# Rotary sine product in one VectorE instruction, and decay factors completed on ScalarE

## The chip, the cores and the metric

The kernel runs on one core of a Trainium2 chip. The time is device microseconds of one execution, the median over repeated runs. The engines are TensorE (PE, with its weight loads PEld), VectorE (DVE), ScalarE (ACT), GpSimd (POOL) and the queue engine SyncE (SP). Each takes its instructions in order, and they wait for each other through semaphores.

## What is computed

The input `x` has 32 sequences of 256 tokens with 256 features, all in float32. A state-space block, conditioned by a vector per sequence, comes first, then two layers of windowed attention with a gated feed-forward, and the input is added to the end. Cut to what the change touches:

```python
# state-space block: one decay factor per state (16) and token
dt = jnp.tanh(dt @ W_dt.T + b_dt) * 0.01
A = -jnp.tanh(A_log)
Ad = 1.0 + dt * A
def step(h, inputs):
    ad, bd, xt, ct = inputs
    h = jnp.clip(h * ad[:, :, None] + bd[:, :, None] * xt[:, None, :], -10.0, 10.0)
    return h, jnp.einsum('bd,bdh->bh', ct, h)
...
# attention: rotary embedding of q and k, heads of 64
def rotate_half(x):
    x1, x2 = jnp.split(x, 2, axis=-1)
    return jnp.concatenate([-x2, x1], axis=-1)
q = q * cos * scale + rotate_half(q) * sin * scale
k = k * cos / scale + rotate_half(k) * sin / scale
```

## The kernel before, in words

The 32 sequences are worked on in 4 groups of 8. The scan of a group takes 256 steps, one per token, in 8 chunks of 32. A step holds the states of 8 sequences x 16 states on 128 partitions and 512 features, and is one VectorE instruction (`step`, L722), which reads the former state and the token's row `xrep`, already spread by a DMA and scaled on ScalarE (`scale_row`, L712); TensorE reads four states out at a time (L734). For each chunk a preparation runs ahead of the steps: convolution (L474 to L514), layer norm and projections, and then the factors of the chunk.

These factors are where the first edit lies. `figures_in` (L636 to L644) makes the inputs `bcd` on VectorE, `decay_th` (L649) takes the tanh of 128x32 values on ScalarE, and `decays` multiplies it by a value per partition and adds 1 on VectorE (L654). A scan instruction (L656) makes the running product `pd`, and L659 to L663 its reciprocal `pi`, the scaled `beta` and `ct`. Each row of the chunk is scaled by `beta` on ScalarE before its step. `decay_th` stands in slot -6 before its chunk and `decays` in slot -5, where a slot is one step of the scan.

The second edit lies in the attention, which works on one sequence after another, for 2 layers. TensorE projects one window of 128 tokens to q or k in a PSUM bank (L996, 128x512: 8 heads of 64). `rotated` squares it on ScalarE (L1009), multiplies it by the cosine table on VectorE (L1012, into `rot`), and then by the sine table with the halves of each head exchanged, in two VectorE instructions of 128x256 (L1017, into `swp`). GpSimd adds the two (L1020). VectorE sums the squares (L1022), GpSimd raises the sums to -1/2 (L1026), and VectorE scales `rot` with that (L1032). That is done 4 x 8 x 2 x 2 x 2 = 256 times. The sign of the rotation is in the sine table. `swp` and the squares share three buffers with the end result `fo`, and a PSUM bank comes free when its last reader, L1017, has ended.

The program text says which slot of the scan and which stage of the attention work stands in: the scan of group 0 runs alone, then the attention of one group runs beside the scan of the next, and the attention of the last group runs alone. But the text is not the order of the queues. A planner takes the instructions at build time and writes each engine's order from its own costs, taking at each point the first in program order that it holds to be ready. `keep_in_program_order` pins some instructions behind their predecessors (L712 in the later groups, L1032). An instruction that is added, dropped or has another cost can so change the order on every engine. Other lines named further on: L588/L589 and L764 are GpSimd products and sums of 128x512, L1423 and L1443 finish the feed-forward on VectorE, L1060 adds the attention's output.

## Time and profile before

| | |
|---|---|
| median of 3 runs | 3534.1 us (3530.1 to 3535.7) |
| the profiled execution | 3535.6 us, span of its instructions 3533.5 us |
| granted TensorE clock | 0.99 of full speed |
| L654, factor on VectorE | 32 x 570 ns |
| L649, tanh on ScalarE | 32 x 318 ns |
| L1012, cosine product, 128x512 | 256 x 684 ns |
| L1017, sine product, 128x256 | 512 x 416 ns |
| L1020, addition on GpSimd, 128x512 | 256 x 1348 ns |
| L722, scan step | 1024 x 896 ns |

A row of the profile names the line, engine, operation, output and inputs, the shapes and the count; behind the bar come the busy time in us, the mean ns of one instruction, then the idle time of its engine just before such instructions and what ended it. The chain of waits goes back from the last instruction, at each step to what released it or to the instruction before it on its engine; "issue" in it is time in which the profile shows nothing that the engine waited for. TensorE's busy time is modelled and covers short gaps.

### The profile page before, as it was taken

The numbers are of one execution on the slowest core, as the hardware profiler recorded it, in microseconds if no ns is written. First come the engines' busy times: TensorE is split into PE (matmuls) and PEld (weight loads), VectorE is DVE, ScalarE is ACT, GpSimd is POOL, SyncE is SP. The second block draws the span as 40 slices with busy tenths as digits, with TensorE's granted clock in tenths as the row PEclk, the third lists the DMA queues.
The fourth block names the chain that finished last, engine by engine and source line by source line (L and its number), as shares of the span: only waits on it lengthen the run. The fifth ranks groups of instructions, "written<-read, shape, count | busy, mean of one in ns | idle before, by whom it ended". The sixth has DMA issues, their size and how long they took to land.

```text
span 3533.5 us, 56484 instructions
## 1 busy us (share of the span) xinstructions
PE 3418.2 (97%) x19580; PEld 2257.4 (64%) x19580; DVE 2683.2 (76%) x5177; ACT 2035.4 (58%) x3663; POOL 1625.6 (46%) x1587
## 2 busy tenths in 40 slices
PE   7999989999999999999999999999999999999999
PEld 4545335666666666666666666666666777777777
DVE  5888898878788788888888888888787655555563
ACT  4666656656666665666666656666566444444442
POOL 4433456544455555544455555544444434333441
PEclk9999999999999999999999999999999999999999
DMA  7787655545454555444454555544444212011111
GB/s 208 215 217 218 198 169 153 136 113 142 129 143 130 150 147 151 136 114 134 117 142 128 148 148 147 137 120 130 118 142 118 61 37 62 13 31 36 37 28 38
DMA packets 487195, 436.65 MB, mean 124 GB/s; under 512 B 247155, under 2 KB 326516, under 8 KB 486772
## 3 DMA queue, kind: packets, MB, share of 16 engines
q1 hardware_dynamic: 401426, 420.41, 42.2%
q10 hardware_dynamic: 85474, 12.53, 2.1%
q8 instruction: 157, 2.57, 0.3%
q14 instruction: 138, 1.13, 0.1%
HBM read 384.06 MB, written 47.19 MB: 122 GB/s over the span
## 4 chain that ended last, share of the span: by engine, by line
PE 63%; DVE 17%; DMA 7%; POOL 5%; ACT 4%; issue 3%; SPq 1%; ACTq 0%; DVEq 0%; POOLq 0%
PE ps_qkv L996 13%; PE pa L1405 13%; DVE h L722 7%; PE po_f L1432 6%; PE y L734 5%; PE ps_wo L1052 4%; PE ov L1289 3%; DMA xrep<-xnd 3%; PE ps_out L814 3%; PE ps_in L401 3%; PE sc L1232 3%; PE tr_qk L1041 2%; PE rs L1269 2%; PE ps_raw L520 2%; DVE acc L491 1%
## 5 line engine op out<-in xcount | busy, mean ns | idle before, releaser
L722 DVE CUSTOM_DVE_ANT_0 h<-h,xrep,lim 128x512 f32<-128x512 f32 x1024 | 917.2, 896 | 137.3 <-ACT xrep L712 93.4
L712 ACT ACTIVATE xrep<-xrep,beta 128x512 f32<-128x512 f32 x960 | 671.6, 719 | 265.5 <-DMA xrep<-xnd 178.2
L996 PE MATMUL ps_qkv<-qkv,res 128*128 128x512 f32 x1536 | 716.0, 601 | 26.6 <-DVE ag L1423 12.5
L1405 PE MATMUL pa<-hT,w 128*128 128x256 f32 (+1 forms) x2816 | 674.7, 382 | 5.1 <-DVE zT L805 5.1
L1405 PEld LDWEIGHTS pa<-hT,w 128*128 128x128 f32 (+1 forms) x2816 | 517.4, 188 | 145.4 <-issue 41.8
L1020 POOL TENSOR_TENSOR rot<-rot,swp 128x512 f32<-128x512 f32 x256 | 345.1, 1348 | 496.7 <-DVE swp L1017 465.9
L996 PEld LDWEIGHTS ps_qkv<-qkv,res 128*128 128x128 f32 x1536 | 282.0, 191 | 311.5 <-issue 247.0
L1026 POOL TENSOR_TENSOR rn<-ss,neg_half 128x8 f32<-128x8 f32 x256 | 457.6, 1788 | 0.0
L734 PE MATMUL y<-h,ly 128*32 128x512 f32 x2048 | 341.1, 606 | 15.7 <-DVE h L722 13.6
L1432 PE MATMUL po_f<-ag,w 128*128 128x256 f32 x1280 | 306.7, 387 | 3.8 <-DVE fo L1443 3.1
L1423 DVE SCALAR_TENSOR_TENSOR ag<-pa,b_sb,ag 128x256 f32<-128x256 f32 x320 | 151.5, 474 | 208.7 <-ACT ag L1416 208.7
L1009 ACT ACTIVATE sq<-ps_qkv,tiny 128x512 f32<-128x512 f32 x256 | 173.3, 685 | 186.3 <-PE ps_qkv L996 129.3
L1432 PEld LDWEIGHTS po_f<-ag,w 128*128 128x128 f32 x1280 | 235.3, 190 | 68.3 <-DVE pT L1260 12.9
L1416 ACT ACTIVATE ag<-pa,b_sb 128x256 f32<-128x256 f32 x320 | 150.0, 469 | 209.7 <-PE pa L1405 206.8
L1357 POOL TENSOR_TENSOR rstd<-ve,neg_half 128x2 f32<-128x2 f32 x64 | 46.5, 726 | 484.9 <-DVE ve L1355 484.8
L1052 PE MATMUL ps_wo<-oT,wo 128*128 128x256 f32 x1024 | 231.6, 379 | 0.0
L1012 DVE TENSOR_TENSOR rot<-ps_qkv,rc_sb 128x512 f32<-128x512 f32 x256 | 175.1, 684 | 71.8 <-ACT sq L1009 70.1
L491 DVE SCALAR_TENSOR_TENSOR acc<-xr,wc_sb,acc 128x256 f32<-128x256 f32 x384 | 183.1, 499 | 50.8 <-POOL acc L480 50.0
L1017 DVE TENSOR_TENSOR swp<-ps_qkv,rs_sb 128x256 f32<-128x256 f32 x512 | 191.8, 416 | 27.6 <-POOL rot L1020 27.5
L1052 PEld LDWEIGHTS ps_wo<-oT,wo 128*128 128x128 f32 x1024 | 194.5, 190 | 27.2 <-ACT th_g L774 0.8
L1032 DVE SCALAR_TENSOR_TENSOR rot<-rn,rot 128x512 f32<-128x512 f32 x256 | 205.7, 841 | 7.5 <-POOL rn L1026 7.5
L1244 ACT ACTIVATE pT<-sc 128x512 f32<-128x512 f32 x384 | 201.6, 601 | 8.2 <-PE sc L1232 6.1
(161 smaller groups left out, 5375.6 us busy)
## 6 DMA issues: line engine op xcount, KB each, us to landing
xrep<-xnd SPq DMA_DIRECT2D x960, 256.0 KB
rb<-inv SPq DMA_DIRECT2D x128, 256.0 KB
xnd<-xn SPq DMA_DIRECT2D x64, 256.0 KB
qkv<-in_wqkv_dram SPq DMA_DIRECT2D x24, 512.0 KB
ahead<-xs_a SPq DMA_DIRECT2D x48, 256.0 KB
xp<-ahead SPq DMA_DIRECT2D x48, 256.0 KB
xd<-xnd SPq DMA_DIRECT2D x192, 64.0 KB
w<-in_w_dram SPq DMA_DIRECT2D x80, 128.0 KB
```

The source lines that it names most:

```text
L491: nc.vector.scalar_tensor_tensor(acc, xr[:, :, k : k + CH], wc_sb[:, ch, k : k + 1], acc, ALU.mult, ALU.add,)
L712: scaled = nc.scalar.activation(bx, ck[c].pop(("bx", t), bx), AF.Copy, scale=ck[c]["beta"][:, t : t + 1])
L722: nc.vector._custom_dve(TENSOR_ADD_SAT, out=h_new, in0=state["h"], in1=bx, s0=ck[c]["lim"][:, 0, t : t + 1], s1=ck[c]["lim"][:, 1, t : t + 1],
L734: nc.tensor.matmul(ck[c]["y", hb][32 * q : 32 * q + 32, :], ly[hb % 2][:, 32 * t : 32 * t + 32], ck[c].pop(("h", hb * TB + t)), start=(i = ...
L996: nc.tensor.matmul(ps, res[b][:, k, t0 : t0 + W], wt["qkv", a][:, k], start=(k == 0), stop=(k == KM - 1),)
L1020: nc.gpsimd.tensor_add(rot, rot, swp)
L1026: nc.gpsimd.tensor_tensor(rn, ss, neg_half, ALU.pow)
L1032: nc.vector.scalar_tensor_tensor(rot, bc(rn, 2, DH), 1e12, rot, ALU.min, ALU.mult)
L1052: nc.tensor.matmul(po[:, d], wt["wo", 0][:, c, d * P : (d + 1) * P], oT[:, c, :], start=(c == 0), stop=(c == NC_ - 1),)
L1244: nc.scalar.activation(p, banks[r], AF.Exp)
L1405: nc.tensor.matmul(dst[x], wt["w1", m][:, k, x], self.h[:, k], start=(k == 0), stop=(k == KM - 1),)
L1432: nc.tensor.matmul(self.po[:, d], wt["w2", 0][:, m, d * P : (d + 1) * P], self.ag[m], start=(m == 0), stop=(m == len(MCH) - 1),)
```

## The change

The two sine products become one of 128x512. It reads the PSUM bank as (head, half, 32) with the halves backwards, and the table and the output in their plain order. And ScalarE computes `1 + a * tanh` itself, in place, in an activation (Identity, with a scale and a bias per partition) directly behind the tanh; VectorE's instruction for it is gone.

```diff
             def decay_th(c):
                 ad = sm.tile([P, CH], FP, tag="ad", name="ad")
                 nc.scalar.activation(ad, ck[c]["bcd"][:, 2], AF.Tanh, bias=wbias[:, 2:3])
+                nc.scalar.activation(ad, ad, AF.Identity, bias=one, scale=a_sb)
                 ck[c]["ad"] = ad
 
             def decays(c):
                 ad, bcd, beta = ck[c].pop("ad"), ck[c].pop("bcd"), ck[c]["beta"]
-                nc.vector.tensor_scalar(ad, ad, a_sb, 1.0, ALU.mult, ALU.add)
...
             hd = DH // 2
-            for i in range(2):
-                o, s = slice(i * hd, (i + 1) * hd), slice((1 - i) * hd, (2 - i) * hd)
-                nc.vector.tensor_mul(
-                    swp[:, :, o], ph[:, :, s], bc(rs_sb[:, l, w, a, o], 1, HEADS)
-                )
+
+            nc.vector.tensor_mul(
+                swp.rearrange("p h (i d) -> p h i d", i=2),
+                ps.rearrange("p (h i d) -> p h i d", h=HEADS, i=2)[:, :, ::-1, :],
+                bc(rs_sb[:, l, w, a].rearrange("p (i d) -> p i d", i=2), 1, HEADS),
+            )
```

## The prediction

> **What bounds the kernel now.** I read the page's busy shares first, then the busy time by stage, then the chain of waits through one period of the middle stage, and last the timeline of VectorE (DVE) around the lines that change.

> ```profile
> PE 3418.2 (97%) x19580; PEld 2257.4 (64%) x19580; DVE 2683.2 (76%) x5177; ACT 2035.4 (58%) x3663; POOL 1625.6 (46%) x1587
> ```

> The second view is the busy time of each engine in three stretches (PE, PEld, DVE, ACT, POOL in that order, then the granted clock, the DMA share and GB/s).

> ```profile
> 100.00:400.00 300.00, 283.86 (x1244) 149.95 (x1242) 261.19 (x455) 195.77 (x360) 115.61 (x156) 0.95 0.79 217
> 1700.00:2600.00 900.00, 879.26 (x5165) 593.63 (x5162) 748.16 (x1474) 558.67 (x1020) 453.55 (x423) 1.00 0.48 134
> 2700.00:3500.00 800.00, 799.97 (x4711) 581.60 (x4704) 448.59 (x861) 356.73 (x606) 297.20 (x234) 1.00 0.16 42
> ```

> There are three stages. Behind 2700 us TensorE (PE) has no gap at all, so nothing that VectorE saves there counts. In the middle PE idles 20.7 of 900 us (2.3%), and from 100 to 400 us 16.1 of 300. Over the whole span it idles 3533.5 - 3418.2 = 115 us, and that is the most that a faster VectorE could ever return. The middle repeats itself every 100 us, once per chunk of the scan. Its chain of waits (start, length, what) has these pieces:

> ```profile
> 1744.76 0.72 DVE h L722
> 1745.48 0.09 DVE ad L654
> 1745.57 1.00 issue
> 1746.57 0.80 DVE h L722
> 1747.37 0.20 DVE pd L656
> ...
> 1765.10 0.60 DVE rot L1012
> 1765.70 0.67 DVE swp L1017 x2
> 1766.38 0.03 issue
> 1766.40 0.02 POOLq L1020
> 1766.42 0.09 issue
> 1766.51 1.28 POOL rot L1020
> 1767.79 0.02 issue
> 1767.81 0.07 DVE swp L1017
> ```

> Both edited lines are on the chain: the decay's L654, and the sine products L1017 with the GpSimd addition L1020 that waits for them. Summing the chain's pieces by line over the whole span gives 39.2 us for L1017 (120 pieces) and 3.6 us for L654 (19 pieces). So the change touches the path that sets the end, but little of it.

> **Part 1, the sine product.** The duration of a row is not its price, because one VectorE instruction starts before the one in front has ended. The timeline (start, length) shows it:

> ```profile
> 1765.03 0.68 DVE L1012 TENSOR_TENSOR rot<-ps_qkv,rc_sb 128x512 f32<-128x512 f32 x1
> 1765.63 0.73 DVE L1017 TENSOR_TENSOR swp<-ps_qkv,rs_sb 128x256 f32<-128x256 f32 x2
> 1766.29 0.67 DVE L1022 TENSOR_REDUCE ss<-sq 128x8 f32<-128x512 f32 x1
> ```

> The two halves hold the engine from 1765.63 to 1766.29, 0.66 us. The cosine product L1012 has the same sources (PSUM and a broadcast table in SBUF) and 512 elements, and holds it from 1765.03 to 1765.63, 0.60 us. The new instruction is a product of that size, so one pair saves 0.06 to 0.07 us; over all rows the mean start-to-start time is 333 ns for a half, and 600 to 609 ns for a whole L1012. I take 0.066 us, or 17 us of VectorE in 256 pairs. On the chain it is 39.2 / 0.333 = 118 halves, 59 pairs, **3.9 us**. No row reads with a negative step. The halves read runs of 32 at a stride now, in 333 ns, like the unbroken 256-element sum L474 (334 to 336 ns), and L805 writes a strided output in 0.60 us, so I give the pattern nothing. By the bare durations, 2 x 416 - 684 = 148 ns a pair, the same 59 pairs would give 8.7 us; that end I keep for the range. What waits behind the pair (L1020's addition, the PSUM bank that the scores' matmuls take) gets its data 0.07 us sooner, inside the same sum. The second product of a window waits for L1020 of the first (0.26 us in the same view) and will still do so.

> [...]

> **Part 2, the decay factor on VectorE.** Its group row and that of the tanh in front of it:

> ```profile
> L654 DVE TENSOR_SCALAR ad<-ad,a_sb 128x32 f32<-128x32 f32 x32 | 18.2, 570 | 8.6 <-ACT ad L649 8.6
> ```

> 570 ns is a mean of two things. 20 of the 32 take 223 to 242 ns, and 10 take 1245 to 1261 ns; in all ten GpSimd had begun L764 (a product of two SBUF tensors) 0.2 to 0.4 us before, and the 1.00 us of "issue" in the chain is this hold. Start to start an undisturbed one costs 0.15 to 0.25 us. On the chain: **3.6 us** over 19 pieces, without the holds. Are the holds gained as well, 10 x 1.0 us? The next instruction on VectorE is the scan step L722, which reads two SBUF tensors and is itself seen between 715 and 1896 ns (median 807). So it can be held too, and would then stand in the same place until L764 ends. I count none of the 10 us and keep them as the far end.

> [...]

> From 100 to 450 us the tanh comes late: L654 waited 0.3 to 2.0 us for it at five chunks and 0.5 at a sixth, together 6.9 us, with step L722, whose input may be ready, standing behind it. Now only the scan L656 waits, and L722 lies between. Bounds: 0 (the step is not ready, its rows still on the DMA queue) and 6.9; neither row is nearer, so I take half, **3.5 us**.

> **Part 3, the factor on ScalarE.** 32 new activations of 128x32. The tanh of the same shape takes 318 ns (L649) and reads the same kind of operands, so +0.32 us each, 10 us of ScalarE in all. A ScalarE instruction directly behind the one that feeds it exists (L574, then L581): its wait for L574 sums to 0.4 us in 64, so none is added. Identity is used by L581 and L1383 already with no table load of its own, so no load either. Queued behind it on ScalarE is the row scaling L712, for which the scan step waits. What covers it: ScalarE waits 3.4 us for L638 in front of the tanh and 3.5 us for L660 a few instructions later, once per chunk, and the tanh is on the chain in only 4 pieces. Cost: 4 x 0.32 = **1.3 us**; if that cover is gone, 32 x 0.32 = 10 us.

> No DMA is issued, removed or moved by any part.

> **Sum.** 3.9 + 3.6 + 3.5 - 1.3 = 9.7 us less. The profiled execution took 3535.6 us (span 3533.5 and about 2 us around it), 1.5 above the median of the three runs shown (3534.1), within their spread. Forecast: 3535.6 - 9.7 = **3526 us**. Faster or slower by over 0.2%, what a measurement of this kernel can tell, means under 3527.0 or over 3541.2 us.

> **The rivals.**

> *Holds and waits go too.* If the holds behind L764 vanish (10 us) as well, the time is 3516. For it: the order of VectorE's queue is set at build time, and another instruction may stand there. Against: L722 stands there in 10 of 10 cases. Chance 0.10.

> *Nothing arrives at the end.* The boundary stretch goes on into waits for DMA (L474 waits 2.1 to 2.5 us for its reload, steps for their rows) and into PE work. If these absorb the saved VectorE time, only the early 3.5 us less ScalarE's 1.3 remain: about 3533. For it: PE is within 2.3% of full. Against: the reload is itself started by an earlier VectorE read, so it moves along. That the edit does nothing it says, the product of 512 costing as much as two of 256, lands here too. Chance 0.20.

> *Late factors.* The planner orders every engine's queue from its own costs. Today the scan stands 1.9 us behind L654's start (1745.40 to 1747.29). With L654 gone from the queue it may be put up to that much earlier, while on ScalarE one row scaling (0.63 us from start to start) may slip between tanh and factor. Then VectorE, in order, stands at the scan: 0.63 + 0.32, about 0.95 us at each of 24 boundaries behind the first group, 23 us; and the step behind it waits along, so no saving of part 2 there. 3535.6 + 23 - 3.9 = 3555 us. It decides from the point at which the scan stands less than 0.95 us behind the tanh's end. For it: VectorE has waited for the tanh already, up to 2.0 us. Against: in the middle the tanh ended 1.15 us before L654 began. Another shift of order that costs about 0.95 us per period would look the same. Chance 0.32.

> **How the numbers follow.** The forecast has 0.38; its own bounds are 3535.6 - 3.9 - 3.6 - 6.9 = 3521 and, with the early term at 0 and ScalarE uncovered, 3535.6 - 7.5 + 10 = 3538. I put 0.30 of it under 3527 and 0.08 within. Faster: 0.30 + 0.10 = 0.40. Same: 0.08 + 0.20 = 0.28. Slower: 0.32. The range runs from 3511, the holds' case with the pairs at 8.7 instead of 3.9 us (3516 - 4.8), to 3556, which takes in the late factors at 0.95 us and leaves out those that cost more, about 0.1; below it about 0.05 is left out.

> **What would show it.** Right: 256 rows of 128x512 at about 684 ns in place of 512 halves; L654 gone; 32 more ScalarE rows of some 320 ns; L1020's wait for swp a little less; PE's gaps between 500 and 2600 us down by a few us in all. Holds passed on: more L722 at 1.7 us and longer. Wrong: sine rows well above 684 ns (the reversed reading costs), waits of the scan L656 for ScalarE, or PE gaps per 100 us that grew.

## The result, and the profile after

The changed kernel takes 3557.0 us (3552.6 to 3560.2, median of 6), the kernel before on the same chip 3531.6 us: ratio 1.0065, 95% interval 1.0052 to 1.0077. The forecast was 3526; the measured time is 1 us above the upper end of the range (3556). The profiled execution took 3560.2 us (span 3558.4). From L1017 on, line numbers of the changed kernel are one higher than before (the addition L1020 is L1021, the gate product L1423 is L1424, its gelu L1416 is L1417), and the one sine product is L1016.

First the page's busy shares of the changed kernel, then its three stretches (PE, PEld, DVE, ACT, POOL, granted clock, DMA share, GB/s).

```profile
PE 3433.6 (96%) x19580; PEld 2259.1 (63%) x19580; DVE 2673.4 (75%) x4889; ACT 2047.7 (58%) x3695; POOL 1619.1 (46%) x1587
```

```profile
100.00:400.00 300.00, 281.25 (x1228) 147.13 (x1227) 256.39 (x439) 195.65 (x363) 114.96 (x151) 0.97 0.78 213
1700.00:2600.00 900.00, 871.74 (x5143) 586.46 (x5142) 736.77 (x1372) 556.27 (x1018) 445.06 (x420) 0.99 0.47 131
2700.00:3500.00 800.00, 800.00 (x4709) 579.55 (x4708) 456.55 (x793) 363.60 (x615) 305.63 (x239) 1.00 0.17 45
```

DVE and ACT did what the edits say: 288 VectorE instructions and 9.8 us of it gone, 32 ScalarE instructions and 12.3 us more. But PE's gaps in the middle grew, from 20.7 to 28.3 of 900 us, and PE's own busy time rose by 15.4 us with the same 19580 matmuls. The edited rows, by form:

```profile
L1016 DVE TENSOR_TENSOR swp<-ps_qkv,rs_sb 128x512 f32<-128x512 f32 x256 | 175.3, 685 | 27.4 <-POOL rot L1021 27.1
L656 DVE TENSOR_TENSOR_SCAN pd<-ad,pd,zero_ch 128x32 f32<-128x32 f32 x28 | 19.0, 678 | 11.8 <-ACT ad L650 11.8
L650 ACT ACTIVATE ad<-ad,one,a_sb 128x32 f32<-128x32 f32 x32 | 13.2, 412 | 1.0
L649 ACT ACTIVATE ad<-bcd,wbias 128x32 f32<-128x32 f32 x32 | 10.2, 317 | 53.3 <-DVE bcd L638 53.3
```

The sine product is as forecast (685 ns beside 684). The factor costs 412 ns, not 320. Comparing the starts of the scan's 32 chunks in both traces, the changed kernel is 8.7 us behind at 439 us, 5.2 at 1255 us, 24.6 at 2656 us, and loses nothing after that. Between 1255 and 2263 us it loses 0.7 to 3.1 us per chunk, at the chunk boundaries. A boundary is here the stretch in which one chunk of steps ends and the factors of the next are made. One of them in the changed kernel, in the chain of waits (start, length, what):

```profile
1759.17 4.85 DMA xrep<-xnd
...
1764.10 0.07 ACT xrep L712
...
1764.73 0.46 ACT ag L1417
1765.19 0.02 issue
1765.22 0.48 DVE ag L1424
1765.70 0.72 DVE h L722
1766.42 0.40 DVE acc L491
1766.82 0.34 DVE xr L474
1767.15 0.03 DVE acc L491
1767.18 4.05 DMA xp<-ahead
```

Read downwards: a row's DMA ends, the row scaling L712 can start, behind it in ScalarE's queue stands the gelu L1417, VectorE's gate product L1424 waits for the gelu, and only after it comes L474, whose read frees the buffer of the reload `xp` (4.05 us). ScalarE's and PE's timelines of the same place (start, length, operation; in brackets the idle time and what ended it):

```profile
1756.35 0.71 ACT L712 ACTIVATE xrep<-xrep,beta 128x512 f32<-128x512 f32 x1
1759.66 0.72 ACT L712 ACTIVATE xrep<-xrep,beta 128x512 f32<-128x512 f32 x1 [2.60 <-DVE beta L660]
1760.29 0.56 ACT L1047 COPY qT<-tr_qk 128x512 f32<-128x512 f32 x1
1760.75 0.59 ACT L1047 COPY kT<-tr_qk 128x512 f32<-128x512 f32 x1
1761.23 0.73 ACT L712 ACTIVATE xrep<-xrep,beta 128x512 f32<-128x512 f32 x1
1764.10 0.72 ACT L712 ACTIVATE xrep<-xrep,beta 128x512 f32<-128x512 f32 x1 [2.14 <-DMA xrep<-xnd]
1764.73 0.46 ACT L1417 ACTIVATE ag<-pa,b_sb 128x256 f32<-128x256 f32 x1
```

```profile
1768.83 1.88 PE L996 MATMUL ps_qkv<-qkv,res 128*128 128x512 f32 x4
1773.92 3.78 PE L996 MATMUL ps_qkv<-qkv,res 128*128 128x512 f32 x4 [3.21 <-DVE ag L1424]
1777.63 1.94 PE L734 MATMUL y<-h,ly 128*32 128x512 f32 x8
```

The same boundary in the kernel before, where it comes 12 us sooner:

```profile
1745.71 0.73 ACT L712 ACTIVATE xrep<-xrep,beta 128x512 f32<-128x512 f32 x1
1746.33 0.47 ACT L1416 ACTIVATE ag<-pa,b_sb 128x256 f32<-128x256 f32 x1
1750.31 0.72 ACT L712 ACTIVATE xrep<-xrep,beta 128x512 f32<-128x512 f32 x1 [3.51 <-DVE beta L660]
1752.68 0.73 ACT L712 ACTIVATE xrep<-xrep,beta 128x512 f32<-128x512 f32 x1 [1.65 <-DMA xrep<-xnd]
```

```profile
1756.87 1.88 PE L996 MATMUL ps_qkv<-qkv,res 128*128 128x512 f32 x4
1760.33 1.98 PE L996 MATMUL ps_qkv<-qkv,res 128*128 128x512 f32 x4 [1.58 <-DVE ag L1423]
```

Two row scalings stand and wait in both, before for 3.51 and 1.65 us. But before, the gelu L1416 is ahead of them; in the changed kernel (2.60 us for `beta`, 2.14 us for a row) the gelu is behind both, and the q/k copies L1047 behind the first. Before, PE gets a hole (a stretch without a matmul) of 1.58 us. In the changed kernel it gets one of 3.21 us, and the four matmuls behind it take 3.78 us where the four before took 1.88: the granted clock is at half (0.50 over 1774 to 1779 us). The clock's mean over 1766 to 1782 us is 0.79; before, over 1766 to 1782 us of its own time, 1.00.

Nothing in the source orders this. Written as lines, the planner's order at 14 chunk boundaries, the first at about 1250 us and the last at 2550 us, is (in the changed kernel's line numbers, the factor L650 added to the old one, L654 left out):

```diff
 ScalarE
-L649 L650 L712 L1047 L1047 L712 L1417 L712 L712 L1278
+L649 L650 L712 L712 L1047 L1047 L712 L712 L1417 L1278
 VectorE
-L722 L722 L656 L1424 L1061 L1033 L1033 L659 L662 L660 L722 L1424 L722 L491 L474 L491
+L722 L656 L722 L659 L662 L660 L1061 L1033 L1033 L1424 L491 L722 L1424 L722 L491 L474
```

(At the first and the last of the 14 it differs by a place or two.) To make the whole old order into the new one, at least 248 of VectorE's instructions that both kernels have must be moved, and 83 of ScalarE's; on the other queues 30 of GpSimd's, 44 of SyncE's and 19 of TensorE's.

### The profile page after: what moved, and what is told of

Read it like the earlier page. It is cut to its first block, busy times and chain, and to the rows that moved or that the text cites. A ratio compares the mean times of both kernels' runs of the same rounds, so it can differ in the third digit from the quotient of the medians.

```text
span 3558.4 us, 56167 instructions
## 1 busy us (share of the span) xinstructions
PE 3433.6 (96%) x19580; PEld 2259.1 (63%) x19580; DVE 2673.4 (75%) x4889; ACT 2047.7 (58%) x3695; POOL 1619.1 (46%) x1587
## 4 chain that ended last, share of the span: by engine, by line
PE 62%; DVE 16%; DMA 9%; POOL 5%; ACT 4%; issue 3%; SPq 0%; ACTq 0%; DVEq 0%; POOLq 0%
PE ps_qkv L996 13%; PE pa L1406 12%; PE po_f L1433 7%; DVE h L722 6%; DMA xrep<-xnd 4%; PE y L734 4%; PE ps_wo L1053 4%; PE ov L1290 4%; PE sc L1233 3%; PE ps_out L814 3%; PE ps_in L401 2%; PE tr_qk L1042 2%; PE rs L1270 2%; DVE acc L491 2%; PE ps_raw L520 1%
## 5 line engine op out<-in xcount | busy, mean ns | idle before, releaser
L722 DVE CUSTOM_DVE_ANT_0 h<-h,xrep,lim 128x512 f32<-128x512 f32 x1024 | 921.0, 899 | 151.1 <-ACT xrep L712 103.9
L712 ACT ACTIVATE xrep<-xrep,beta 128x512 f32<-128x512 f32 x960 | 672.7, 719 | 271.8 <-DMA xrep<-xnd 203.0
L996 PE MATMUL ps_qkv<-qkv,res 128*128 128x512 f32 x1536 | 723.2, 606 | 36.8 <-DVE ag L1424 25.3
L1021 POOL TENSOR_TENSOR rot<-rot,swp 128x512 f32<-128x512 f32 x256 | 340.1, 1329 | 475.7 <-DVE swp L1016 436.7
L734 PE MATMUL y<-h,ly 128*32 128x512 f32 x2048 | 351.2, 613 | 16.9 <-DVE h L722 14.5
L1424 DVE SCALAR_TENSOR_TENSOR ag<-pa,b_sb,ag 128x256 f32<-128x256 f32 x320 | 151.9, 475 | 219.6 <-ACT ag L1417 219.6
L1417 ACT ACTIVATE ag<-pa,b_sb 128x256 f32<-128x256 f32 x320 | 149.7, 468 | 210.9 <-PE pa L1406 207.5
L1012 DVE TENSOR_TENSOR rot<-ps_qkv,rc_sb 128x512 f32<-128x512 f32 x256 | 175.2, 684 | 73.5 <-ACT sq L1009 71.7
L480 POOL TENSOR_SCALAR acc<-xr,wc_sb,bconv_sb 128x256 f32<-128x256 f32 x128 | 99.6, 781 | 272.6 <-DVE xr L474 101.0
L491 DVE SCALAR_TENSOR_TENSOR acc<-xr,wc_sb,acc 128x256 f32<-128x256 f32 x384 | 185.3, 500 | 42.7 <-POOL acc L480 40.7
L1033 DVE SCALAR_TENSOR_TENSOR rot<-rn,rot 128x512 f32<-128x512 f32 x256 | 209.2, 855 | 5.3 <-POOL rn L1027 5.3
```

The costliest lines, as they stand in the source:

```text
L491: nc.vector.scalar_tensor_tensor(acc, xr[:, :, k : k + CH], wc_sb[:, ch, k : k + 1], acc, ALU.mult, ALU.add,)
L712: scaled = nc.scalar.activation(bx, ck[c].pop(("bx", t), bx), AF.Copy, scale=ck[c]["beta"][:, t : t + 1])
L722: nc.vector._custom_dve(TENSOR_ADD_SAT, out=h_new, in0=state["h"], in1=bx, s0=ck[c]["lim"][:, 0, t : t + 1], s1=ck[c]["lim"][:, 1, t : t + 1],
L734: nc.tensor.matmul(ck[c]["y", hb][32 * q : 32 * q + 32, :], ly[hb % 2][:, 32 * t : 32 * t + 32], ck[c].pop(("h", hb * TB + t)), start=(i = ...
L996: nc.tensor.matmul(ps, res[b][:, k, t0 : t0 + W], wt["qkv", a][:, k], start=(k == 0), stop=(k == KM - 1),)
L1021: nc.gpsimd.tensor_add(rot, rot, swp)
```

## The experiments

Theory: the edits save what was forecast, and the new order loses more. Rival: the edits themselves cost the time (late factors, the reversed reading). All ratios are to the kernel before on the same chip, 5 rounds. "Held" means that every engine is tied to a given order by edges between neighbours that the planner must keep; they add no instruction.

| kernel | order | ratio | 95% interval |
|---|---|---|---|
| sine product alone | planner's own | 1.0019 | 1.0007 to 1.0032 |
| decay alone | planner's own | 1.0052 | 1.0033 to 1.0071 |
| both edits | old, held | 0.9978 | 0.9966 to 0.9990 |
| neither edit | new, held | 1.0085 | 1.0063 to 1.0107 |
| neither edit | old, held (control) | 0.9999 | 0.9989 to 1.0010 |
| sine product alone | old, held | 0.9988 | 0.9975 to 1.0001 |
| decay alone | old, held | 0.9980 | 0.9970 to 0.9989 |
| both | new, gelu first at 14 boundaries | 1.0021 | 1.0010 to 1.0031 |
| both | new, ScalarE's queue old | 1.0040 | 1.0025 to 1.0055 |
| both | new, gelu and gate product first | 1.0078 | 1.0065 to 1.0091 |
| both | old, gelu later at 13 boundaries | 1.0033 | 1.0022 to 1.0044 |
| both | old, gelu sooner at 13 boundaries | 0.9975 | 0.9967 to 0.9984 |
| both | new, 14 boundaries old on both engines | 0.9992 | 0.9981 to 1.0003 |
| both | old, 14 boundaries new on both engines | 1.0036 | 1.0022 to 1.0050 |

### Each edit alone, the order left to the planner

The one half of the diff, or the other.

> The one sine product alone; the decay factor stays on VectorE; the planner makes a new order. Theory O (the order makes the loss): anywhere from 3520 to 3560 us, since the order is new again, and the boundary of a chunk tells why; the product itself is worth about -4 us. Theory E (an edit itself costs): if the reversed product is the costly one, about 3557; if the decay factor is, about 3528.

> The decay factor on ScalarE alone; two sine products as before; a new order. Theory O: 3530 to 3565 us, and, as the loss in the first 440 us (where no sine product runs) came with the changed kernel already, this one should show it too: about 9 us later at step 256 than before. Theory E: if the factor on ScalarE is the costly edit, about 3557; if the product is, about 3530.

Measured 1.0019 and 1.0052. Either edit alone makes the planner order the queues anew, and either loses. The decay alone starts its scan's step 256 10.3 us later than before, as expected. These two runs can't tell an edit's cost from that of its order.

### The order taken apart from the edits

```diff
             else:
                 scan_to(lo + (hi - lo) * r // group)
+        _pin(tc)
...
+def _pin(tc):
...
+    for engine, text in ORDER.items():
...
+        for a, b in zip(order, order[1:]):
+            tc.add_manual_dep(
+                made[b], made[a].name,
+                mybir.DependencyInfo(
+                    mybir.DependencyClass.NoSync, mybir.DependencyReason.DATA
+                ),
+                reason="order",
+            )
```

`ORDER` holds the sequence of each engine's instructions in program order numbers. Both edits got the order of before, the code of before got the order of after (L654 directly ahead of its scan, the two halves where the whole stood), and as a control the code of before its own order.

> Both edits, but every engine's instructions pinned to the order of the kernel before (the new activation directly behind its tanh, the one product in the place of the two). Theory O: the loss is gone, 3520 to 3531 us, nearest to 3532 - 8 = 3524. Theory E: about 3557, since the instructions are those of the changed kernel.

> Neither edit, but every engine pinned to the order of the changed kernel (the VectorE factor directly ahead of its scan, the two half products in the place of the one). Theory O: 3555 to 3570 us, the changed kernel's loss and the dearer instructions on top. Theory E: about 3532, since the instructions are those of the kernel before.

> Control: the kernel before, neither edit, every engine held to its own order by the same order edges as the other runs. The edges add no instruction; ratio 1.000, within 0.1%.

Measured 0.9978, 1.0085 and 0.9999. The edges cost nothing. The edits in the old order gain 0.22%; the new order with neither edit loses 0.85%. So the order makes the loss, and the rival, that the edits themselves cost it, is out. Both edits in the old order are also faster than the kernel before and the changed one.

Each edit alone in the old order sizes the terms of the sum:

> The sine product alone, every engine held to the order of the kernel before. By the prediction's sum, 59 pairs on the chain at 0.066 us: -3.9 us, ratio 0.9989. If the shorter product is only passed on as waiting for GpSimd or TensorE: 1.0000. With both edits in the old order at 0.9978 (-7.7 us), what this one brings leaves the rest to the decay.

> The decay factors on ScalarE alone, every engine held to the order of the kernel before. By the prediction's sum: L654 off the chain -3.6 us, early waits -3.5, ScalarE +1.3, in all -5.8 us, ratio 0.9984. By the trace of both edits in the old order, which stood 5 us behind at 440 us, where no sine product runs: the early waits grow instead, +5 us by 440 us, and about -9 us after it if the sine product brings its -3.9; in all -4 us, 0.9989. If VectorE's time is passed on as waiting for the later factor: 1.000 to 1.001.

Measured 0.9988 and 0.9980 of 3533.8 us, 4.2 and 7.1 us less, each with an interval of 3 to 5 us to both sides. Together they would be 11 us; both edits measured 7.8 (0.9978). The intervals take that in. That of the sine product alone ends at 1.0001, so this run by itself doesn't exclude that it brings nothing.

### The gelu's place

In the order of the changed kernel, only this was moved, at 14 boundaries:

```diff
 ScalarE
-L649 L650 L712 L712 L1047 L1047 L712 L712 L1417 L1278
+L649 L650 L712 L712 L1047 L1047 L1417 L712 L712 L1278
```

> Both edits, every engine held to the order of the changed kernel, and at 14 boundaries one thing put back: ScalarE's gelu (L1417) goes in front of the row scalings (L712) that the new order put ahead of it, directly behind the q/k copies. Theory A (gelu behind a late row): the changed kernel loses 5 us up to 840 us and 19 us more from there to 2656 us, 1.3 to 2.7 us per 100-us boundary; the gelu waits about 2 us at each for a scaling whose row is still on its way, VectorE's gate product (L1424) and the reload behind it follow, and TensorE runs at half clock after the hole. With the gelu first about 14 to 19 us of this go: ratio 1.001 to 1.003. Rival B (VectorE's order itself: scan, step parts and unit products L1033 ahead of the gate product): the gate product comes late all the same, and the ratio stays at 1.005 to 1.007.

Measured 1.0021: half of the way from 1.0065 to 0.9978. What PE waited for between 1300 and 2700 us (us in total, times, longest), in the changed kernel and in this one:

```profile
PE ps_qkv L996 <- DVE ag L1424: 25.3, 12, 3.4
PE ps_qkv L996 <- DVE xd L785: 5.5, 8, 0.7
```

```profile
PE sc L1233 <- DVE swp L1016: 11.1, 13, 0.9
PE ps_qkv L996 <- DVE xd L785: 8.9, 13, 0.7
```

With the gelu first, the wait for the gate product is gone from the list, and so are the stretches at half clock there: between 1300 and 2700 us the clock's records have 20.5 us at 0.5 in the changed kernel, 3.4 before, and none here. A part of the wait only moves: PE now stands 11.1 us for the sine product, for which it stood 0.9 us in the changed kernel. Over the scan's steps from the chunk start at 1255 us to that at 2656 us its idle time falls from 40.7 to 31.4 us.

The converse, in the old order:

```diff
 ScalarE
-L649 L650 L712 L1047 L1047 L712 L1417 L712 L712 L1278
+L649 L650 L712 L1047 L1047 L712 L712 L712 L1417 L1278
```

> Both edits, every engine held to the order of the kernel before, which measured 0.9978, and one thing made worse: at 13 boundaries ScalarE's gelu (L1417) goes two places back, behind the two row scalings (L712) that follow it. In the trace of the kernel without this, at the boundary of 1747 us, these two scalings stand 2.8 us waiting for beta (L660) and 1.2 us for a row's DMA, behind the gelu, where it costs nothing. Theory A (whatever stands behind a waiting row scaling in ScalarE's queue is late, and the reload with it): the gelu comes 3 to 5 us later at each of 13 boundaries; of that 2 to 4 us reach the end: 26 to 50 us, ratio 1.005 to 1.012. Rival B (the loss comes from VectorE's order and the place of the gelu matters little): 0.998 to 1.000.

Measured 1.0033, 0.55% above 0.9978: 19 us in 13 boundaries, 1.5 us each. The direction is theory A's; the price is below its 2 to 4 us. The way to PE is another one than in the changed kernel: between 1300 and 2700 us its projections stand 0.4 us for the gate product in place of 25.3 us, and its longest waits are

```profile
PE sc L1233 <- DVE swp L1016: 9.5, 11, 0.9
PE ps_qkv L996 <- ACT qT L1047: 9.4, 10, 1.6
```

And one place sooner:

```diff
 ScalarE
-L649 L650 L712 L1047 L1047 L712 L1417 L712 L712 L1278
+L649 L650 L712 L1047 L1047 L1417 L712 L712 L712 L1278
```

> Both edits, every engine held to the order of the kernel before (0.9978), and at 13 boundaries ScalarE's gelu one place sooner, ahead of the row scaling that stands between it and the q/k copies. That scaling has its row and its beta there, and takes 0.7 us. If 0.7 us of the gelu reach the reload at every boundary: -9 us, ratio 0.995 to 0.996. If the gelu is early enough once it stands behind no waiting scaling: 0.9973 to 0.998.

Measured 0.9975, the same as 0.9978 within the intervals: a gelu that stands behind no waiting scaling is early enough. It has the lowest ratio of the table, without a difference to both edits in the old order that could be told.

### One engine's order without the other's

> Both edits, VectorE, GpSimd, SyncE and TensorE held to the order of the changed kernel, ScalarE alone to the order of the kernel before. Theory A (gelu behind a late row, ScalarE's queue alone): ratio 1.001 to 1.003, as for the kernel with the gelu put first, and the loss of 5 to 9 us in the first 440 us stays. Rival B (VectorE's order): 1.005 to 1.007. A third case: with VectorE's order new and ScalarE's old, VectorE waits for operations that the old order of ScalarE brings later, and the ratio is above 1.0065.

Measured 1.0040, between both theories: by the chunk starts it falls 7.4 us further behind between 778 and 1357 us, where the changed kernel loses nothing, and is level behind 1357 us. ScalarE's old queue helps at the late boundaries and hurts at earlier ones. There VectorE stands 5.3 us in two waits for a tanh of the convolution (L506 on ScalarE), which are not in the changed kernel: the third case of the text above, at these places only.

For the next one the gelu stayed first, and on VectorE the gate product was put back ahead of the residual, the unit products and the rest of the recurrence, at the first 13 of the 14 boundaries and at one at 673 us:

```diff
 VectorE
-L656 L722 L659 L662 L660 L1061 L1033 L1033 L1424
+L722 L656 L1424 L1061 L1033 L1033 L659 L662 L660
```

> Both edits, the order of the changed kernel with the gelu first at 14 boundaries (measured 1.0021), and at the same boundaries on VectorE the gate product (L1424) put back in front of the residual and unit products (L1061, L1033) and of the rest of the recurrence (L659 to L660). If VectorE's order at these boundaries is what is left of the loss: as with the whole old order, 0.998 to 0.9995. If the rest of the loss lies elsewhere (the first 440 us, the boundaries between 500 and 1300 us, other queues): 1.001 to 1.002.

Measured 1.0078: neither, worse than with the gelu alone. PE's waits of this kernel between 1300 and 2700 us, and ScalarE's:

```profile
PE ps_qkv L996 <- ACT qT L1047: 20.2, 12, 2.1
PE sc L1233 <- DVE swp L1016: 11.2, 13, 0.9
```

```profile
ACT xrep L712 <- DVE beta L660: 56.3, 13, 4.8
ACT xrep L712 <- DMA xrep<-xnd: 47.0, 24, 3.1
```

With L660 later on VectorE, the row scalings wait for `beta` 13 times, up to 4.8 us (20.9 us in 8 waits with the gelu first alone), and PE waits 20.2 us for the q/k copies, which the new order has behind such a scaling (1.9 us with the gelu first alone). It is the same mechanism at another place: what stands behind a waiting scaling is late.

### Both engines at the 14 boundaries together

The two orders of the first diff above, swapped at these 14 places alone, in the rest of the new order and in the rest of the old one (the first place is at about 1250 us, where the text has 1350):

> Both edits, every engine held to the order of the changed kernel, but at the 14 boundaries from 1350 us on VectorE and ScalarE together in the order of the kernel before. If all of the middle's loss lies in the order of these two engines at these places: about 1.3 to 2.7 us back at each, about what the kernel with both edits in the old order has behind 1350 us, and only the few us from the first 440 us and from other boundaries stay: ratio 0.9985 to 1.000. If the gelu's place was all that these places cost: 1.002, as with the gelu first alone. If the order elsewhere (other engines too) counts: above 1.002.

> The converse: both edits, every engine held to the order of the kernel before (0.9978), but at the same 14 boundaries VectorE and ScalarE together in the order of the changed kernel. If these places make the loss: +1.3 to 2.7 us at each, ratio 1.003 to 1.007. If the loss needs the rest of the changed order too: 0.998 to 1.000.

Measured 0.9992 and 1.0036. Of the 0.87% between both edits in the old order and in the new one, these 14 places make 0.73% taken out and 0.58% put in. PE's waits for the gate product follow them, with the old boundaries first and the new ones second:

```profile
PE ps_qkv L996 <- DVE ag L1424: 8.2, 11, 1.4
```

```profile
PE ps_qkv L996 <- DVE ag L1424: 23.6, 12, 3.2
```

One length in the traces goes with the loss in these kernels: from the start of the tanh L649 to the start of the next sum L474, whose read lets the reload `xp` start. Means over the first 13 of the 14 boundaries, and the time from the chunk start at 1255 us (times of the kernel before) to that at 2656 us:

| kernel | L649 to gelu, us | L649 to L474, us | the 14 chunks, us |
|---|---|---|---|
| before | 2.4 | 8.2 | 1401.8 |
| changed | 7.7 | 9.7 | 1421.2 |
| both, old order held | 2.9 | 8.1 | 1397.4 |
| both, new, ScalarE's queue old | 2.9 | 8.5 | 1405.0 |
| both, new, gelu first | 5.5 | 8.8 | 1406.0 |
| both, new, gelu and gate product first | 7.4 | 10.8 | 1427.3 |
| both, old, gelu later | 7.8 | 9.9 | 1419.5 |
| both, new, 14 boundaries old | 2.9 | 8.1 | 1395.8 |
| both, old, 14 boundaries new | 7.8 | 9.8 | 1418.8 |

From the kernel before to the changed one the reload starts 1.5 us later, 13 times, which is 19 us; the chunks take 19.4 us longer. The loss follows the start of the reload also where the gelu's place alone doesn't give it. That is read from the traces; no run moved the reload's start by itself.

What is left, 0.14 to 0.29%, lies in the rest of the new order and is hardly more than the intervals. The first 440 us, where the scan L656 waits for the factor, is a possible place, but single profiles differ there by 5 us and more with the order alike, and it was not taken apart. A seventh buffer for the rows, which might take the waiting away and leave the order, was not run.

## Why the prediction was wrong, point by point

**The step that failed** is the choice of case. The forecast (0.38) took the order of the queues as before, and so did its sum. The sum has no term for a new order. The planner's order changed, and the runs put that term at 0.87%, 31 us (both edits: 0.9978 in the old order, 1.0065 in the planner's own), against 7.8 us of savings that arrived. The third rival had a changed order at 0.32, with "another shift of order that costs about 0.95 us per period would look the same". That its price, 3555 us, is near the measured 3557 is luck, for its place was another: it had VectorE standing at the scan L656 for a late factor at 24 boundaries. The scan waits for L650 only early:

```profile
DVE pd L656 <- ACT ad L650: 10.5, 7, 2.8
```

That is the first 480 us of the changed kernel; over the whole span it is 12.1 us in 9 waits. Of the prediction's signs of being wrong two showed, these waits and PE gaps that grew, but the larger loss isn't in the first. The loss between 1255 and 2263 us comes from the order on ScalarE and VectorE around the scan, and the instruction that it makes late is not one that the edits touch. The prediction saw this chain's pieces (the reload started by an earlier VectorE read) and used them only as an argument that a saving moves along. It works the other way as well.

**How the middle's loss adds up.** From the chunk start at 1255 us to that at 2656 us the changed kernel takes 19.4 us longer. Over the same steps PE's idle time rose by 10.9 us (29.8 to 40.7), and the clock's records have 17.1 us more at half speed, in which PE gets about half its work done (four matmuls in 3.78 us there, in 1.88 us at full speed): an estimate of up to 8.5 us. The two together are as long as the loss, but that doesn't show the split: with the gelu later in the old order the same steps took 17.7 us longer than before, with 11.4 us more of idle time and no more half speed, so a part can also lie in short gaps that the modelled busy time covers. The prediction counted holes in PE at their own length, and took PE's 115 us of idle time for the most that could be returned. In the trace some holes cost more than their length (behind the 3.21 us of the boundary above, four matmuls took 1.90 us longer).

**Part 1, the sine product: right.** 685 ns a row, no price for the reversed reading, -4.2 us alone in the old order where the sum had -3.9. That run's interval ends at 1.0001, so its time alone doesn't show the gain. The start-to-start times do, for VectorE's own saving: 602 ns from one sine product to the next instruction, where the two halves took 2 x 333 ns, 64 ns less.

**Part 2, the decay on VectorE: about right.** Alone in the old order it gave 7.1 us less where parts 2 and 3 sum to 5.8. The waits for the tanh, of which 3.5 us were to go, fell from 8.6 to 4.4 us (now for L650) in that run, and grew to 12.1 in the new order. The holds passed on as forecast, but not only to L722. In the changed kernel the scan stands there at 11 chunks, each time with L764 running on GpSimd:

```profile
1757.15 1.28 DVE L656 TENSOR_TENSOR_SCAN pd<-ad,pd,zero_ch 128x32 f32<-128x32 f32 x1
```

Eleven scans take over 1 us (one before). With both edits in the old order it is L722, which takes 1.52 us directly ahead of the scan at 1743 us, and whose count at 1.2 us and longer goes from 95 to 105 (that at 1.7 us and longer, which the prediction named, doesn't rise: 15 and 13). In the changed kernel that count is 106 beside the eleven scans, so it doesn't show by itself where a hold went. By the ten L654 before (1.25 to 1.26 us) and the eleven scans (up to 1.30 us), the hold belongs to the place, not to the instruction. The 10 us were worth nothing: with them the decay alone would have gained some 16 us in the old order, and its interval ends at 11.

**Part 3, the factor on ScalarE: mis-sized.** 0.41 us instead of 0.32, and 0.35 from the tanh's start to its own. 12.3 us of ScalarE in place of 10; where the order is kept, no cost beyond the sum's 1.3 us shows within that run's interval. The prediction read the factor's operands as the same kind as the tanh's. The tanh has one value per partition (its bias), the factor two (scale and bias), and a pair of rows of the kernel before differs in the same way: of two activations of 128x256 from PSUM, L1416 with one takes 469 ns, L1383 with two 560. Their functions differ too, and no run here changed the operands alone.

**The other rivals.** The holds did not vanish; a saving that doesn't arrive is refuted by 0.9978 in the old order.

## What to carry to other kernels

Where a planner writes the queues, an edit of ten microseconds is priced in two parts: its own sum, and what any new order may do; run the edit in the old order (and the old code in the new one) before judging it. In an in-order queue, look for instructions that wait (here row scalings for a DMA or for `beta`) and ask what stands behind them and which transfer hangs on that; two engines' orders have to fit, and a half of a good order can lose again what another half had gained (1.0021 to 1.0078). A kernel that gained in the old order should be shipped with that order held.

## What the runs showed of the hardware

What decides in these traces is where a hole lies. In each trace the changes of the clock between 100 and 2800 us are whole multiples of 3.413 us apart (to within 5 ns), so they lie on a grid. In the changed kernel each of the 12 records follows a stretch of that grid in which PE idled for 1.91 us or more; the two holes without a record are cut by the grid, and leave 1.85 and 1.92 us in their longer parts. In all sixteen traces, between 470 and 2700 us, there are 67 stretches at full clock with 2.0 us or more of idle time, and half clock follows all 67; of the other 10,251 it follows 13. So a hole of 2 to 3 us costs nothing behind its end or up to half of a record, 1.7 us or more (an estimate from the records of 3.41 us and up), by where it falls. The stretch from 1766 to 1782 us in the changed kernel (columns as above) has such a one, its granted clock at 0.79:

```profile
1766.00:1782.00 16.00, 12.79 (x54) 5.91 (x53) 12.61 (x29) 9.77 (x17) 5.08 (x10) 0.79 0.51 119
```
